# Waits of a few turns, shared products in a gradient, and the dealing out of expert units in a hand-scheduled two-layer network

## The chip, the cores and the metric

The kernel runs on one core of one Trainium2 chip. The metric is the device time of one execution in microseconds (us). The kernel before takes 3922.72 us, the median of three runs (3920.65 to 3936.18). All shares and durations below come from one further execution with the profiler, which took 3921.06 us.

## What is computed

Two residual layers over x of 16 sequences by 512 tokens by 128 features, in float32. Each layer normalises its input once and adds two branches to it:

```python
x = x + memory(xn) + block(xn)            # layer 0, xn = layernorm(x)
x = x + attention2(xn) + moe32(xn)        # layer 1
```

- `memory`: a neural memory. Keys k and values v come from the tokens. Over eight chunks of 64 tokens, one after the other, a two-layer network (w0, w1, and a norm weight ln) predicts v from k; its loss is differentiated by hand, the gradient is clipped to norm 1 over all parameters, and the parameters take a step with momentum. Then all tokens are read out through the final network.
- `block`: a convolution over three tokens, attention with 16 heads of 8 features (not causal), a layernorm, and eight dense experts of width 512, all applied to all tokens and weighted by a softmax gate.
- `attention2`: causal attention, a convolution over its output whose result is used as queries for a second causal attention with the same keys and values, and a projection.
- `moe32`: 32 experts of width 96, the best eight per token, with a capacity of 128 tokens per expert.

With the forward pass y = h w1ᵀ, r = 1/rms(y), ŷ = y r, pred = k + ŷ ln, and e = (pred - v) = ŷ ln + (k - v), the gradient of a chunk needs, per token (th is the token's step weight):

```
for y:   r * th * (e*ln - ŷ * mean(e*ln*ŷ))
for ln:  sum over tokens of th * e * ŷ
```

## The kernel before

The work of all sequences and both layers is cut into generators (`norm0`, `scan`, `front0`, `tops`, `back`, `post0`, `ffn`, `middle`, `front1`, `between`, `last`, `moe`). The class `Turns` runs them: in each **turn** every live generator goes on to its next `yield`, in the order of a priority number (`tops` is 0, `back` 1, the memory 3, the rest 4 to 6). Instructions are issued in that order, and TensorE (PE) keeps it; the other engines' orders are the scheduler's. The last argument of `idle(n)` is a number of turns, and a transfer or a chain on slow engines is covered by idling.

- `largest` (lines 371 to 420, in `tops`) computes the attention scores of a sequence and half of the heads once, only for the row maxima: per turn eight or fewer matmuls into one PSUM tile `s`, and VectorE (DVE) takes the maximum into `nm` (L396, or L387 with the causal mask). There is one such tile, so the next turn's matmuls (`s<-kx,qx`) wait for DVE. In the causal case the rows of keys are 512, 384, 256 and 128 wide; the two narrow ones put two or four heads into a turn and add the mask on the last 128 columns in two additions (L395) before the maximum. DVE instructions of later priority stand behind the maximum of their turn.
- The maxima go through DRAM (`top`) into extra rows of `qx`. `back` starts `lag` turns after `tops` has marked this, computes the scores anew with the maxima subtracted (`s<-qx,kx`), exponentiates on ScalarE (ACT), masks on GpSimd (POOL, L471) and sums against the values (`pc<-e,vp`).
- `ffn(b)` (line 511) runs the dense experts of sequence b as 64 **units**: `first` is a matmul `phe` with its relu, `second` four matmuls into `pye`. A credit of TURN minus the modelled load of the turn's other matmuls, at most 4000, buys units at 1000 each; with `pairs` only even numbers are taken, and none or four while the values of a turn are being summed. At the start it loads `ac`, `x1T` and expert 0's weights, and idles two turns.
- `fill` (line 195) puts a matmul without use into a turn whose PE load is light, if no unit was due in the last two turns.
- `scan` is the memory: `project(c)` makes keys and values of a chunk, `step(c)` a chunk's update. In it `gradient(q)` treats one half of the tokens (L860 to L898: L878 on POOL, L880 to L894 on DVE, L897 on ACT), the halves starting at turns 7 and 11 of the step. `norm_gradient` (L900) starts at turn 16 and makes the products for ln over all tokens on POOL (L904 to L910) in the buffer `gy`, which it shares with the loaded tokens `xc` of a chunk. `readout(b)` starts every six turns once the steps are done; `rq` goes through POOL (L1000, L1001) before PE transposes it, and its `yq` lies in the one buffer `hT1` until its sum is stored.
- Layer 1 starts when the scan is done; turns are counted from `t0`, 44 per sequence. `middle(b)` needs `ffn(b)` done, `front1(b)` loads `xT`, which `middle` has stored to DRAM just before, and idles two turns.
- All plain transfers are issued from SyncE's (SP's) queue, in order: one that waits holds up those behind it.

```python
credit[0] = min(credit[0] + TURN - load_ns[0], 4000)
n = int(max(credit[0] + 500, 0) // 1000)
if pools["pairs"]:
    n = n // 2 * 2 if "values" not in locks or n > 3 else 0
```

Of the kernel before, what the change touches and what calls it, by code (L numbers as in the profile page):

```python
# [17 lines left out]
P = 128  # L18
# [13 lines left out]
NTILE = N // P  # L32
BASE_LR = 0.01

TURN = 2750

ARRAY = 860
SCALE = 1.0 / float(np.sqrt(DH))
# [35 lines left out]
def bc(ap, axis, n):  # L74

    u = ap.unsqueeze(axis)
    shape = list(u.shape)
    shape[axis] = n
    return u.to_broadcast(shape)
# [3 lines left out]
def network(ctx: ExitStack, tc: tile.TileContext, a, out):  # L83
# [181 lines left out]
    def idle(n):  # L265
        for _ in range(n):
            yield
# [102 lines left out]
    def largest(slot, causal):  # L370


        q, k, at = slot
        yield from acquire("p1")
        nm = att.tile([P, TB, 2, NH], F32, tag="nm", bufs=2, name="nm")
        for i, n, per, t in widths(causal):
            qt = TB - 1 - i
            s = pools["ps"].tile([P, 2, 512], F32, tag="p1", bufs=pools["p1"], name="s1")
            sv = s[:, :, 0 : per * n].rearrange("p r (i n) -> p r i n", i=per)
            for u in range(per):  # L380
                for r in range(2):
                    rr = slice(64 * r, 64 * r + 64)
                    mm(sv[:, r, u, :], q[rr, t + u, qt * P : (qt + 1) * P], k[rr, t + u, :n])
            if causal and per == 1:

                for r in range(2):
                    newest[0] = nc.vector.tensor_tensor_reduce(  # L387
                        out=sv[:, r, 0, :], in0=sv[:, r, 0, :], in1=row["caus"][:, S - n :], scale=1.0, scalar=-BIG,
                        op0=ALU.add, op1=ALU.max, accum_out=nm[:, qt, r, t : t + 1],
                    )  # L390
            else:
                if causal:
                    for r in range(2):
                        dg = sv[:, r, :, n - P : n]
                        nc.vector.tensor_tensor(dg, dg, bc(row["caus"][:, S - P :], 1, per), ALU.add)  # L395
                newest[0] = nc.vector.tensor_reduce(nm[:, qt, :, t : t + per], sv, AX.X, ALU.max)  # L396
            yield
        locks.remove("p1")
        padded = maxima.pop(0)
        maxima.append(padded)  # L400
        mp = padded[:, 0 : TB * 16].rearrange("p (t r i x) -> p t r i x", t=TB, r=2, i=2)
        nc.vector.tensor_scalar(mp[:, :, :, 0, :].bitcast(FR), nm, -1.0, None, ALU.mult)
        nc.vector.scalar_tensor_tensor(
            mp[:, :, :, 1, :].bitcast(FR), nm, -1.0, mp[:, :, :, 0, :], ALU.mult, ALU.subtract
        )
        yield
        yield from room()

        tp = work("tpm")
        nc.tensor.transpose(tp[:, 0:P], padded, ident)  # L410
        m = att.tile([TB * 16, P], FR, tag="m", bufs=1, name="m")
        nc.scalar.copy(m, tp[0 : TB * 16, 0:P])
        nc.sync.dma_start(at, m.bitcast(F32))
        at = at.rearrange("(a r i t) s -> r i t a s", r=2, i=2, t=NH)
        for r in range(2):
            rows = q[64 * r + 32 : 64 * r + 34, :, :].bitcast(F32)
            nc.sync.dma_start(rows.rearrange("i t (a s) -> i t a s", s=P), at[r])
        yield
# [87 lines left out]
        mm(o[:, 0 : S - 1], w(2), src[:, 1:S], start=False)  # L506


    credit = [0.0]

    def ffn(b):

        yield from after(("x1", b))
        ac = ff.tile([P, TB, D], F32, tag="x1", bufs=1, name="ac")
        nc.sync.dma_start(flat(ac), x1d[0, b])
        x1T = ff.tile([P, S], F32, tag="x1T", bufs=1, name="x1T")
        nc.sync.dma_start(x1T, x1d[1, b])
        w1, w2 = {}, {}

        def fetch1(e):  # L520
            w1[e] = ff.tile([P, DFF], F32, tag="ew1", bufs=2, name="ew1")
            nc.sync.dma_start(w1[e], a["ew1"][:, e, :])

        def fetch2(e):
            w2[e] = ff.tile([P, 4, D], F32, tag="ew2", bufs=2, name="ew2")
            nc.sync.dma_start(w2[e], a["ew2"][:, e])

        fetch1(0)
        fetch2(0)
        yield from idle(2)  # L530
        pr = sm.tile([P, TB, EXP0], F32, tag="pr", bufs=2, name="pr")
        prT = ff.tile([EXP0, S], F32, tag="y", bufs=2, name="prT")

# [31 lines left out]
            nc.gpsimd.tensor_tensor(ac, ac, y, ALU.add)  # L565
            yield

        hs, pye = {}, [None]

        def first(i):  # L570
            e, f = divmod(i, 4)
            if e + 1 < EXP0 and f < 2:
                (fetch1, fetch2)[f](e + 1)
            ph = work("phe")
            mm(ph, w1[e][:, f * P : (f + 1) * P], x1T)
            hs[i] = ff.tile([P, S], F32, tag="hTe", bufs=3, name="hTe")
            nc.scalar.activation(hs[i], ph, AF.Relu, bias=col("fb", i))  # L577

        def second(i):
            e, f = divmod(i, 4)  # L580
# [12 lines left out]
                nc.gpsimd.tensor_tensor(ac, ac, y, ALU.add)  # L593
                drop()

        n = 4 * EXP0
        units = [(first, 0)]
        for i in range(1, n):
            units += [(first, i), (second, i - 1)]
# [2 lines left out]
        while at < len(units):  # L602

            at_ffn[0] = clock[0]
            credit[0] = min(credit[0] + TURN - load_ns[0], 4000)
            n = int(max(credit[0] + 500, 0) // 1000)
            if pools["pairs"]:
                n = n // 2 * 2 if "values" not in locks or n > 3 else 0
            for fn, u in units[at : at + n]:

                if held[0] >= pools["work"] - (fn is second and u % 4 == 0):
                    break
                fn(u)
                at += 1
                credit[0] -= 1000
            next(gating, None)
            yield
# [139 lines left out]
    def scan(s1):  # L757
# [47 lines left out]
        def step(c):  # L805
# [1 line left out]
            k, kv = ks.pop(c)  # L807

            eb = s1.tile([P, 2 * INTER + D], F32, tag="eb", name="eb")
            ln2 = sm.tile([P, D], F32, tag="ln2", bufs=2, name="ln2")  # L810

            def before():
                nc.gpsimd.tensor_tensor(ln2, ln, ln, ALU.mult)
                yield from idle(4)
                for s_, m_, lo, hi in ((surp, mem, 0, 2 * INTER), (sln, ln, 2 * INTER, 2 * INTER + D)):
                    nc.gpsimd.tensor_scalar(s_, s_, eta[:, c : c + 1], None, ALU.mult)
# [44 lines left out]
            def gradient(q):  # L861


                a4 = slice(4 * q, 4 * q + 4)
                yield from room()
                py = toks(work("py"))
# [8 lines left out]
                gt = s1.tile([P, 2, 4, D], F32, tag=f"hT{q}", name="gt")  # L875
                gq, tq = gt[:, 0], gt[:, 1]
                g[q] = gq
                nc.gpsimd.tensor_tensor(tq, kv[:, a4, :], bc(ln, 1, 4), ALU.mult)  # L878
                yield from idle(3)
                nc.vector.tensor_tensor(yq, yq, bc(ry[:, a4], 2, D), ALU.mult)  # L880
                nc.gpsimd.tensor_tensor(tr[:, a4], ry[:, a4], th[:, a4, c], ALU.mult)
                yield
                nc.vector.tensor_tensor(gq, yq, bc(ln2, 1, 4), ALU.mult)
                yield
                nc.vector.tensor_tensor(gq, gq, tq, ALU.add)
                yield
                nc.vector.tensor_tensor(tq, gq, yq, ALU.mult)
                yield
                nc.vector.tensor_reduce(m[:, a4], tq, AX.X, ALU.add)
                nc.vector.tensor_scalar(m[:, a4], m[:, a4], -1.0 / D, None, ALU.mult)  # L890
                yield
                nc.vector.tensor_tensor(tq, yq, bc(m[:, a4], 2, D), ALU.mult)
                yield
                nc.vector.tensor_tensor(gq, gq, tq, ALU.add)  # L894
                yield
                for t in range(4):
                    nc.scalar.mul(gq[:, t, :], gq[:, t, :], tr[:, 4 * q + t : 4 * q + t + 1])  # L897
                yield  # L898

            def norm_gradient():  # L900

                yield from after(("read", c + 1) if c + 1 < NC else ("read", c))
                gy = late["gy"] = s1.tile([P, NT, D], F32, tag="gy", name="gy")
                nc.gpsimd.tensor_tensor(gy, yh, bc(ln, 1, NT), ALU.mult)  # L904
                yield
                nc.gpsimd.tensor_tensor(gy, gy, kv, ALU.add)
                yield
                nc.gpsimd.tensor_tensor(gy, gy, yh, ALU.mult)
                yield
                nc.gpsimd.tensor_tensor(gy, gy, bc(th[:, :, c], 2, D), ALU.mult)  # L910
                yield

            def back(q):
# [11 lines left out]
                (0, before()), (0, turned(kT, lambda t: k[:, t, :], 0)), (1, turned(kT, lambda t: k[:, 4 + t, :], 1)),  # L925
                *[(1 + q, hidden(q)) for q in range(4)],
                *[(4 + 2 * q + i, hidden_turned(q, i)) for q in range(2) for i in range(2)],
                (7, gradient(0)), (11, gradient(1)), (16, norm_gradient()),
            )
            dyT = s1.tile([P, NT * P], F32, tag="kT", name="dyT")  # L930
            yield from timed(
# [58 lines left out]
        def readout(b):  # L990
# [8 lines left out]
            rms_rows(rq, q, TB, s1)  # L999
            nc.gpsimd.tensor_tensor(q, q, bc(row["qn"], 1, TB), ALU.mult)  # L1000
            nc.gpsimd.tensor_tensor(q, q, bc(rq, 2, D), ALU.mult)  # L1001
            yield from idle(3)
            yield from room()
            qT = s1.tile([P, S], F32, tag="sg", bufs=2, name="qT")
            transpose_tokens(qT, q)
# [18 lines left out]
                for i in range(2):  # L1024
                    mm(py[:, t, :], hT[:, i, t * P : (t + 1) * P], w1T[:, i, :], start=(i == 0), stop=(i == 1))
            ry = sm.tile([P, TB], F32, tag="r_yq", name="r_yq")
            y = s1.tile([P, TB, D], F32, tag="hT1", name="yq")
            nc.scalar.copy(y, py)
            rms_rows(ry, y, TB, s1)
            yield from idle(3)  # L1030
# [55 lines left out]
        mark("tops", layer, b, i, c)  # L1086

    def back(layer, b, i, c):
        yield from after(("tops", layer, b, i, c), lag=4)
        yield from after(("vals", layer, b))  # L1090
        z = live[layer, b]
        if c == 0:
            z["cn"] = (l1 if layer else fa).tile([P, TB, D], F32, tag="cn", bufs=2, name="cn")
        yield from weighted(z[i, c], z["vp"], c, layer == 1, z["cn"], ("back", layer, b, i, c))
# [129 lines left out]
    def front1(b):  # L1224
# [3 lines left out]
        z = live[1, b] = {"vp": got[0]}  # L1228
        xT = l1.tile([P, S], F32, tag="st", bufs=2, name="xT")
        nc.sync.dma_start(xT, xt[1, b])  # L1230
        yield from idle(2)
        for n, order in (("q", (0, 0, 1, 1)), ("k", (0, 1, 0, 1))):
            yield from room()
            pj = hold("pj" + n)
# [219 lines left out]
        nc.sync.dma_start(out_b[b], x1)  # L1454
        yield

    TBB, t0 = 44, max(turns.turn, 480)

    def begun(b, i, c):

# [132 lines left out]
```

## Time and profile before

| | |
|---|---|
| median of three runs | 3922.72 us |
| profiled execution | 3921.06 us |
| its span, first to last instruction | 3919.1 us |
| mean granted PE clock | 0.960 |
| fills: matmuls and their time | 238 matmul records, 122.5 us |
| transfers of SP's queue | 359.73 MB, 32.1% of 16 DMA engines |

The page gives each engine's busy time and its share of the span, and the span in 40 slices with a digit for the busy tenths. A float32 matmul leaves two records, so counts of PE are about twice those of the code. A group row reads: line, engine, operation, result <- operands, shapes, count, then busy time, mean ns of one, and the idle time of the engine just before, with what ended it. A row of waits reads: engine and what waited <- what ended the wait: total us, times, longest. A row of windows gives start and end, length, busy time and count of PE, of its weight loads (PEld), of DVE, ACT and POOL, then the granted clock of PE, the share of the DMA engines and GB/s.

Placed over the trace by the order of PE's instructions, the start takes until 110 us, the memory's eight steps until about 1288 us (turn 400), the readout until 1585 us (turn 482), layer 1 with the last dense experts until 3480 us (turn 1127), and the sparse experts with the last attention the rest. There are 1276 turns.

### The profile page before, as it was taken

What the parts mean: (1) busy time and instruction counts of PE and PEld (TensorE: products, weight loads), DVE (VectorE), ACT (ScalarE), POOL (GpSimd) and SP (SyncE); (2) the same over time, 40 slices, a digit from 0 to 9 for tenths busy, and PEclk for the clock granted to TensorE, in tenths of its full rate; (3) what the DMA queues carried; (4) which work ended last, traced back from release to release, by engine and by line L of the source; (5) the groups of instructions that cost most, each with busy time, mean ns of one, the idle gap of its engine ahead of it and who ended that gap; (6) DMA issues with size and microseconds to landing.
All of it is one profiled execution on the core that took longest, in us unless ns stands there. A gap on an engine that the chain in (4) does not pass through costs nothing. (4 is left out here: it accounts for less than half of the span.)

```text
span 3919.1 us, 62028 instructions
## 1 busy us (share of the span) xinstructions
PE 3463.3 (88%) x22267; PEld 1898.2 (48%) x22267; DVE 2389.2 (61%) x5187; ACT 2152.6 (55%) x3687; POOL 1658.1 (42%) x2562
## 2 busy tenths in 40 slices
PE   5889888889899888999999999999999999987877
PEld 2445444445444444445555555555555555543343
DVE  5666646665665545546466666666666666667762
ACT  1555655665566666555555555555555555543443
POOL 5433542453342544323344344424443344333674
PEclk7999999999999999999999999999999999998998
DMA  5222212221322332433434433443334333433343
GB/s 159 64 64 70 67 51 80 64 67 39 106 69 87 95 86 77 128 87 104 123 94 117 113 112 102 110 122 111 104 107 121 107 113 101 120 97 84 83 91 86
DMA packets 289938, 370.50 MB, mean 95 GB/s; under 512 B 46008, under 2 KB 141408, under 8 KB 289248
## 3 DMA queue, kind: packets, MB, share of 16 engines
q1 hardware_dynamic: 282464, 359.73, 32.1%
q0 software_dynamic: 7168, 6.82, 1.1%
q8 instruction: 176, 2.88, 0.3%
q14 instruction: 130, 1.06, 0.1%
HBM read 236.59 MB, written 133.25 MB: 94 GB/s over the span
## 5 line engine op out<-in xcount | busy, mean ns | idle before, releaser
L467 ACT ACTIVATE e<-s 128x1024 f32<-128x1024 f32 (+1 forms) x1216 | 1190.7, 979 | 702.7 <-PE s L192 637.0
L396 DVE TENSOR_REDUCE nm<-s 128x2 f32<-128x1024 f32 (+1 forms) x704 | 861.2, 1223 | 683.9 <-PE s L192 676.3
L387 DVE CUSTOM_DVE_ANT_0 s<-s,sb_const 128x512 f32<-128x512 f32 (+1 forms) x1024 | 647.6, 632 | 543.1 <-PE s L192 524.3
L471 POOL TENSOR_SCALAR_AFFINE_SELECT e<-e 128x128 f32<-128x128 f32 (+2 forms) x1408 | 467.8, 369 | 1003.2 <-ACT e L467 1000.9
L192 PE MATMUL s<-kx,qx 64*128 64x512 f32 (+3 forms) x3072 | 622.0, 432 | 236.8 <-DVE nm L396 132.1
L192 PEld LDWEIGHTS s<-kx,qx 64*128 64x128 f32 x3072 | 275.2, 188 | 895.6 <-issue 275.3
L192 PE MATMUL pc<-e,vp 128*32 128x512 f32 (+3 forms) x6144 | 642.3, 506 | 26.9 <-POOL e L471 26.5
L585 PEld LDWEIGHTS pye<-ew,hTe 128*128 128x128 f32 x4096 | 514.7, 195 | 141.4 <-issue 126.0
L585 PE MATMUL pye<-ew,hTe 128*128 128x128 f32 x4096 | 581.7, 286 | 0.8 <-DMA ew<-in_ew 0.8
L577 ACT ACTIVATE hTe<-phe,sb_cols 128x512 f32<-128x512 f32 x512 | 353.7, 691 | 404.7 <-PE phe L192 402.8
L192 PE MATMUL phe<-x1T,ew 128*128 128x512 f32 x1024 | 538.4, 610 | 14.1 <-DMA x1T<-x1d 6.7
L192 PE MATMUL s<-qx,kx 64*128 64x512 f32 (+3 forms) x3072 | 511.3, 359 | 34.3 <-ACT e L467 25.7
L593 POOL TENSOR_TENSOR ac<-ac,y 128x512 f32<-128x512 f32 x128 | 164.8, 1288 | 399.7 <-ACT y L592 397.4
L192 PEld LDWEIGHTS s<-qx,kx 64*128 64x128 f32 x3072 | 290.3, 190 | 77.1 <-ACT e L467 54.6
L395 DVE TENSOR_TENSOR s<-s,sb_const 128x256 f32<-128x256 f32 (+1 forms) x384 | 199.9, 521 | 150.8 <-PE s L192 138.4
L192 PEld LDWEIGHTS pc<-e,vp 128*32 128x32 f32 x6144 | 151.9, 110 | 255.8 <-issue 172.9
L192 PEld LDWEIGHTS phe<-x1T,ew 128*128 128x128 f32 x1024 | 160.2, 196 | 32.4 <-issue 8.2
L592 ACT ACTIVATE y<-pye,pr 128x128 f32<-128x128 f32 x512 | 146.6, 369 | 42.7 <-PE pye L585 37.9
L387 DVE DVE_READ_ACCUMULATOR2_ANT nm<- 128x1 f32 x1024 | 144.7, 141 | 0.0
L199 PE MATMUL fill<-sb_pb,sb_const 128*128 128x512 f32 (+2 forms) x238 | 122.5, 603 | 10.8 <-DMA sb_pb<-in_pb 10.4
L205 POOL TENSOR_SCALAR rs_t<-ss 128x4 f32<-128x4 f32 (+1 forms) x56 | 12.0, 215 | 197.4 <-ACT sq L258 195.8
L967 POOL TENSOR_TENSOR cl<-cl,phalf 128x1 f32<-128x1 f32 x8 | 4.5, 568 | 190.1 <-ACT cl L966 190.1
(294 smaller groups left out, 3991.8 us busy)
## 6 DMA issues: line engine op xcount, KB each, us to landing
ew<-in_ew SPq DMA_DIRECT2D x256, 256.0 KB
kx<-rk SPq DMA_DIRECT2D x192, 256.0 KB
qx<-rq SPq DMA_DIRECT2D x128, 256.0 KB
rq<-hi SPq DMA_DIRECT2D x64, 256.0 KB
rq<-lo SPq DMA_DIRECT2D x64, 256.0 KB
rk<-hi SPq DMA_DIRECT2D x64, 256.0 KB
rk<-lo SPq DMA_DIRECT2D x64, 256.0 KB
qx<-r SPq DMA_DIRECT2D x64, 256.0 KB
```

The costliest lines, as they stand in the source:

```text
L192: nc.tensor.matmul(o, lhsT=lhsT, rhs=rhs, start=start, stop=stop)
L199: nc.tensor.matmul(o[:, 0:n], lhsT=ident, rhs=cell[0][:, 0:n], start=True, stop=True)
L205: nc.gpsimd.tensor_scalar(t, src, scale, eps, ALU.mult, ALU.add)
L387: newest[0] = nc.vector.tensor_tensor_reduce(out=sv[:, r, 0, :], in0=sv[:, r, 0, :], in1=row["caus"][:, S - n :], scale=1.0, scalar=-BIG, ...
L395: nc.vector.tensor_tensor(dg, dg, bc(row["caus"][:, S - P :], 1, per), ALU.add)
L396: newest[0] = nc.vector.tensor_reduce(nm[:, qt, :, t : t + per], sv, AX.X, ALU.max)
L467: nc.scalar.activation(e[:, :, 0 : per * n], s[:, :, 0 : per * n], AF.Exp, scale=SCALE)
L471: cleared[0] = nc.gpsimd.affine_select(out=ev[:, r, :, 0:P], in_=ev[:, r, :, 0:P], pattern=[[0, per], [1, P]], compare_op=ALU.is_ge, fill= ...
L577: nc.scalar.activation(hs[i], ph, AF.Relu, bias=col("fb", i))
L585: nc.tensor.matmul(pye[0][:, t, :], lhsT=h[:, t * P : (t + 1) * P], rhs=w2[e][:, f, :], start=(f == 0 and t == 0), stop=(f == 3), skip_gro ...
L592: nc.scalar.mul(y[:, t, :], pye[0][:, t, :], pr[:, t, e : e + 1])
L593: nc.gpsimd.tensor_tensor(ac, ac, y, ALU.add)
```

## The change

- TURN falls from 2750 to 2700.
- The two mask additions of a turn become one of twice the size.
- `fetch0(b)` loads `x1T` and expert 0's weights. It is called when the last `first` of the sequence before has been issued, if the input of the next is ready; only the first sequence fetches for itself, and idles three turns.
- The gradient forms e = ŷ ln + (k - v) once per half, and both results use it: e·ŷ is written into `gy` (for ln, then scaled by th on POOL) and times ln into the mean; e·ln takes the rest. The products of `norm_gradient`, of `ln2` and of (k - v)·ln go; the second half starts at turn 9 instead of 11, and the scaling on ACT one turn later.
- `readout` idles five turns for `rq` instead of three, and its `yq` lies in the buffer of its own hidden values (`h` or `ds`).
- `back` waits five turns behind `tops` instead of four, `front1` three for `xT` instead of two, and `t0` is 480 instead of the turn in which the scan ended, if that is later.

```diff
-TURN = 2750
+TURN = 2700
...
-                    for r in range(2):
-                        dg = sv[:, r, :, n - P : n]
-                        nc.vector.tensor_tensor(dg, dg, bc(row["caus"][:, S - P :], 1, per), ALU.add)
+                    dg = sv[:, :, :, n - P : n]
+                    nc.vector.tensor_tensor(dg, dg, bc(bc(row["caus"][:, S - P :], 1, per), 1, 2), ALU.add)
...
+    def fetch0(b):
+
+        x1T = ff.tile([P, S], F32, tag="x1T", bufs=1, name="x1T")
+        nc.sync.dma_start(x1T, x1d[1, b])
+        fetched[b] = x1T, {}, {}
+        fetch1(*fetched[b][1:], 0)
+        fetch2(*fetched[b][1:], 0)
...
-        fetch1(0)
-        fetch2(0)
-        yield from idle(2)
+        if b not in fetched:
+            fetch0(b)
+            yield from idle(3)
+        x1T, w1, w2 = fetched.pop(b)
...
+            if i == n - 1 and ("x1", b + 1) in done:
+                fetch0(b + 1)
...
-                nc.gpsimd.tensor_tensor(ln2, ln, ln, ALU.mult)
...
-                nc.gpsimd.tensor_tensor(tq, kv[:, a4, :], bc(ln, 1, 4), ALU.mult)
...
-                nc.vector.tensor_tensor(gq, yq, bc(ln2, 1, 4), ALU.mult)
-                yield
-                nc.vector.tensor_tensor(gq, gq, tq, ALU.add)
-                yield
-                nc.vector.tensor_tensor(tq, gq, yq, ALU.mult)
-                yield
+                nc.vector.tensor_tensor(gq, yq, bc(ln, 1, 4), ALU.mult)
+                yield
+                nc.vector.tensor_tensor(gq, gq, kv[:, a4, :], ALU.add)
+                yield from after(("read", c + 1) if c + 1 < NC else ("read", c))
+                if q == 0:
+                    late["gy"] = s1.tile([P, NT, D], F32, tag="gy", name="gy")
+                gy = late["gy"][:, a4, :]
+                yield
+                nc.vector.tensor_tensor(gy, gq, yq, ALU.mult)
+                yield
+                nc.vector.tensor_tensor(tq, gy, bc(ln, 1, 4), ALU.mult)
+                yield
+                nc.gpsimd.tensor_tensor(gy, gy, bc(th[:, a4, c], 2, D), ALU.mult)
                 nc.vector.tensor_reduce(m[:, a4], tq, AX.X, ALU.add)
                 nc.vector.tensor_scalar(m[:, a4], m[:, a4], -1.0 / D, None, ALU.mult)
                 yield
+                nc.vector.tensor_tensor(gq, gq, bc(ln, 1, 4), ALU.mult)
+                yield
                 nc.vector.tensor_tensor(tq, yq, bc(m[:, a4], 2, D), ALU.mult)
-                yield
                 nc.vector.tensor_tensor(gq, gq, tq, ALU.add)
+                yield
                 yield
...
-            def norm_gradient():
-
-                yield from after(("read", c + 1) if c + 1 < NC else ("read", c))
-                gy = late["gy"] = s1.tile([P, NT, D], F32, tag="gy", name="gy")
-                nc.gpsimd.tensor_tensor(gy, yh, bc(ln, 1, NT), ALU.mult)
-                yield
-                nc.gpsimd.tensor_tensor(gy, gy, kv, ALU.add)
-                yield
-                nc.gpsimd.tensor_tensor(gy, gy, yh, ALU.mult)
-                yield
-                nc.gpsimd.tensor_tensor(gy, gy, bc(th[:, :, c], 2, D), ALU.mult)
...
-                (7, gradient(0)), (11, gradient(1)), (16, norm_gradient()),
+                (7, gradient(0)), (9, gradient(1)),
...
-            yield from idle(3)
+            yield from idle(5)
...
-            y = s1.tile([P, TB, D], F32, tag="hT1", name="yq")
+            y = s1.tile([P, TB, D], F32, tag=("h", "ds")[b % 2], name="yq")
...
-        yield from after(("tops", layer, b, i, c), lag=4)
+        yield from after(("tops", layer, b, i, c), lag=5)
...
-        yield from idle(2)
+        yield from idle(3)
...
-    TBB, t0 = 44, max(turns.turn, 480)
+    TBB, t0 = 44, 480
```

More of the change, by code (lines that the diff above doesn't have):

```diff
@@ L506, in conv, with fetch1, fetch2 @@
         mm(o[:, 0 : S - 1], w(2), src[:, 1:S], start=False)
-    credit = [0.0]
+    credit, fetched = [0.0], {}
+    def fetch1(w1, w2, e):
+        w1[e] = ff.tile([P, DFF], F32, tag="ew1", bufs=2, name="ew1")
+        nc.sync.dma_start(w1[e], a["ew1"][:, e, :])
+    def fetch2(w1, w2, e):
+        w2[e] = ff.tile([P, 4, D], F32, tag="ew2", bufs=2, name="ew2")
+        nc.sync.dma_start(w2[e], a["ew2"][:, e])
+    def fetch0(b):
[4 more added lines that the diff above has]
+        fetch2(*fetched[b][1:], 0)
     def ffn(b):
@@ L515, in ffn @@
         nc.sync.dma_start(flat(ac), x1d[0, b])
[L516 to L526, printed above, removed]
-        fetch1(0)
-        fetch2(0)
-        yield from idle(2)
+        if b not in fetched:
+            fetch0(b)
+            yield from idle(3)
+        x1T, w1, w2 = fetched.pop(b)
         pr = sm.tile([P, TB, EXP0], F32, tag="pr", bufs=2, name="pr")
@@ L566, in gate @@
             yield
-        hs, pye = {}, [None]
+        hs, pye, n = {}, [None], 4 * EXP0
         def first(i):
@@ L572, in first @@
             if e + 1 < EXP0 and f < 2:
-                (fetch1, fetch2)[f](e + 1)
+                (fetch1, fetch2)[f](w1, w2, e + 1)
             ph = work("phe")
@@ L594, in second @@
                 drop()
-        n = 4 * EXP0
         units = [(first, 0)]
@@ L605, in ffn @@
             credit[0] = min(credit[0] + TURN - load_ns[0], 4000)
-            n = int(max(credit[0] + 500, 0) // 1000)
+            more = int(max(credit[0] + 500, 0) // 1000)
             if pools["pairs"]:
-                n = n // 2 * 2 if "values" not in locks or n > 3 else 0
-            for fn, u in units[at : at + n]:
+                more = more // 2 * 2 if "values" not in locks or more > 3 else 0
+            for fn, u in units[at : at + more]:
                 if held[0] >= pools["work"] - (fn is second and u % 4 == 0):
@@ L809, in step @@
             eb = s1.tile([P, 2 * INTER + D], F32, tag="eb", name="eb")
-            ln2 = sm.tile([P, D], F32, tag="ln2", bufs=2, name="ln2")
             def before():
-                nc.gpsimd.tensor_tensor(ln2, ln, ln, ALU.mult)
                 yield from idle(4)
@@ L891, in gradient @@
                 yield
+                nc.vector.tensor_tensor(gq, gq, bc(ln, 1, 4), ALU.mult)
+                yield
                 nc.vector.tensor_tensor(tq, yq, bc(m[:, a4], 2, D), ALU.mult)
+                nc.vector.tensor_tensor(gq, gq, tq, ALU.add)
                 yield
-                nc.vector.tensor_tensor(gq, gq, tq, ALU.add)
                 yield
```

## The prediction

> **What bounds it now.** I read the page first, the busy line and the slices:
>
> ```profile
> PE 3463.3 (88%) x22267; PEld 1898.2 (48%) x22267; DVE 2389.2 (61%) x5187; ACT 2152.6 (55%) x3687; POOL 1658.1 (42%) x2562
> ...
> PE   5889888889899888999999999999999999987877
> ...
> PEclk7999999999999999999999999999999999998998
> ```
>
> TensorE (PE) is the bound throughout: 456 us of the span of 3919.1 are left idle, and no other engine passes 61%. The page's chain of work that ended last covers only the last 43 us (indirect scatters, final copies), so it can't price the middle. A gain has to come out of PE's idle time, its fill matmuls, or its clock. Second, PE's waits over the whole span ("waited for: total us, times, longest"):
>
> ```profile
> PE s L192 <- DVE nm L396: 132.1, 145, 5.9
> ...
> PE pjq L192 <- DMA xT<-xt: 11.5, 7, 5.0
> ...
> PE tp L244 <- POOL rq L1001: 9.8, 4, 4.7
> ...
> PE s L192 <- DMA qx<-top: 7.8, 5, 2.7
> PE phe L192 <- DMA x1T<-x1d: 6.7, 1, 6.7
> ...
> PE pgt L192 <- DMA x1T<-x1d: 4.3, 2, 3.5
> PE tp L244 <- ACT yq L1028: 4.3, 1, 4.3
> PE ppq L192 <- ACT yq L1028: 4.2, 1, 4.2
> ```
>
> Each of these rows stands in front of something that the diff edits. Third, the windows behind single waits; PEclk is the granted clock, next to last but two:
>
> ```profile
> 1646.00:1658.00 12.00, 6.17 (x12) 2.40 (x13) 4.23 (x16) 2.74 (x3) 0.00 (x0) 0.59 0.40 130
> 1676.00:1686.00 10.00, 3.45 (x6) 1.55 (x6) 0.85 (x1) 1.63 (x2) 0.00 (x0) 0.66 0.94 274
> ...
> 2560.00:2570.00 10.00, 7.96 (x54) 3.75 (x57) 6.39 (x28) 3.10 (x4) 2.08 (x6) 0.83 0.63 206
> ```
>
> Here PE waited 5.04 us (from 1645.9, xT), 6.74 us (from 1675.8, x1T) and 1.82 us (from 2560.4, xT). Afterwards part of the window runs at a lower clock: (1 - 0.59) x 12 = 4.9 us, 3.4 us and 1.7 us are lost on top. So a wait of about 2 us or more is paid nearly twice. The mean clock of 0.960 says that this loss is 157 us in all.
>
> **Transfers** (lag 4 to 5; xT three turns ahead instead of two; x1T and expert 0's weights fetched by the batch before). The rows: 11.5 + 6.7 + 4.3 + 7.8 = 30.3 us of idle; the clock loss behind the six longest, from windows like the above, 4.9 + 3.4 + 3.4 + 1.8 + 1.7 + 1.7 = 17; together 47. A turn of this stage lasts 2.92 us on average, more than every xT and top wait but the 5.04, of which about 2 us stay. x1T now starts when the last `phe` matmul of the batch is through, not behind SyncE's (SP's) wait for the accumulator's store. In the new order of SP's instructions it stands ahead of that store. I take 35 of 47. The added waits: `lag` delays the weighting of each pair of heads by one turn, which only keeps a score slot longer; the turns in which score rows are produced stay the same in the order of instructions, up to the last, and the end comes one turn later (1277 turns for 1276): +2.
>
> A rule speaks against counting the clock: the Trainium skill (TensorE: Matmul & The Clock Gate, HAM oscillation) says to avoid PE gaps above about 3.4 us, and the wait at 2560 of 1.82 us is followed by 0.83 all the same. By the rule only the waits of 5.04, 6.74 and 3.45 us would lose clock, 12 us in place of 17. The measurement decides; I keep 17.
>
> **Readout** (five idle turns instead of three; `y` in the tile of its own hidden values instead of the single hT1). Rows: 9.8 + 4.3 + 4.2 and smaller ones behind yq of 2.4, 20.7 us; clock loss in the five windows 1326:1340, 1399:1412, 1438:1452, 1488:1498, 1550:1566: 3.4 + 3.4 + 3.4 + 1.7 + 5.1 = 17. Of 38 I take 30. Two more turns give POOL some 7 us more; the wait for a tile whose store is pending goes, as its next user comes some nine turns later. What the turns cost: the scan ends at turn 486 instead of 482, which is hidden by the attention of layer 0, whose turns run on; layer 1's first rows are ready at turn 513 instead of 507 and are used from 544.
>
> **Gradient.** The longest waits for the maxima (nm) lie here. The timeline at 597 us, with start, duration, engine, line:
>
> ```profile
> 597.41 2.68 POOL L906 TENSOR_TENSOR gy<-gy,v 128x1024 f32<-128x1024 f32 x1
> ...
> 597.80 2.84 DVE L883 TENSOR_TENSOR gt<-yh,ln 128x512 f32<-128x512 f32 x1
> ...
> 600.57 1.21 DVE L396 TENSOR_REDUCE nm<-s 128x2 f32<-128x1024 f32 x1
> ...
> 601.83 0.50 PE L192 MATMUL s<-kx,qx 64*128 64x512 f32 x2 [2.32 <-DVE nm L396]
> ```
>
> and the groups of VectorE (DVE) in 110 to 1288 us (busy, mean ns, then idle before):
>
> ```profile
> L883 DVE TENSOR_TENSOR gt<-yh,ln 128x512 f32<-128x512 f32 x16 | 28.7, 1794 | 0.0
> ...
> L920 DVE TENSOR_TENSOR ds<-ds,pdh 128x512 f32<-128x512 f32 x32 | 21.5, 677 | 0.0
> ```
>
> A product of two SBUF tiles takes 0.68 us alone and up to 2.84 us beside a product on POOL; one with an operand in PSUM (L920) stays at 0.68. The maxima queue behind it, and PE behind them. The change removes POOL's L904 to L908 (19.9 + 21.5 + 21.5), L910 (17.3), L878 (21.3) and L813 (3.6): 105 us; it adds 16 scalings of 512 elements at 1.06 us (the row of L1001), 17. DVE's six products per quarter cost 115.4 us over 96 calls, 1.20 each; now there are eight, 128 calls at between 0.68 and 1.20: 87 to 154. I take 0.80, as projection's POOL products (L797 to L801) still collide. What this frees on PE: the eight longest stalls of the stage (185, 202, 332, 444, 600 to 607, 737, 1007, 1131) sum to 30 us, and 19 more of clock; a wait of 3.98 us at 872 behind the scaling on ScalarE (L897, which now gets one more turn) with 1.7 of clock; 55 in all. Against it: the second half starts at turn 9 instead of 11, so both chains stand in DVE's queue for some eight turns of a step. At 0.68 the new order puts at most 2.5 us between two maxima in a running step, which with 1.22 for the maximum exceeds a turn's 3.3. I take 25 of 55.
>
> **Mask.** Two additions become one. By the rows L395, two of 256 elements (0.43 each) become one of 512 (0.70), two of 512 one of 1024 (1.22, the reduce's row): 0.17 us off DVE's chain per turn, 192 turns. In 121 of them a PE gap ends with this chain, at most 20 us; I take 10.
>
> **Experts.** I cut both instruction orders into turns, counted the units and gave the counts the mean times of before. Turns 540 to 1120: 284 without a unit (2.53 us), 233 with two (2.93), 63 with four (4.67); after 279, 242, 59: 1695.4 against 1690.5, -5. The same for turns 110 to 540: -13. The last unit moves from turn 1125 to 1133: turns 1120 to 1145 get 12 more units, +4; -14 together. Twelve fills fewer (119 to 107; 122.5 us / 119 = 1.03 each) all lay in the empty turns between batches, which shrink from 5 to 8 to 3 to 6. Since some of those idle times are counted above, -13 for the whole. TURN's 2% alone moves little, because units go out in pairs.
>
> **New waits.** A shifted order draws its accidental waits anew. Those of before that the change doesn't aim at (4.59 us at 286, 2.23 us at 554, each with 3.4 of clock) make 13.6; I add 13.
>
> **Sum**: -35 + 2 - 30 - 25 - 10 - 13 + 13 = -98. Against the profiled execution (3921.06 us, 2 more than its span) 3823; the median shown lies 1.7 higher: **3825 us**.
>
> **Rivals.** *The waits return elsewhere*: half of each term survives, since DVE's queue or the next transfer is only a little less late: about 3870. For it: PE's waits for nm L396 number 145, most of them short and untouched. *More comes true*: 47 + 38 + 55 + 20 + 14 + 12 (fills) with nothing new, less 2, make 184: 3739; no row speaks for a schedule without new waits, but 3780 is half-way. *It does not do what it says*: pairs make TURN's change void and the batches' ends are all that move: that loses only the 13, 3838. *Slower, SP's queue*: the prefetch puts a wait for the last `phe` and for weights into SP's in-order queue, ahead of score rows. SP already waits 297.5 us in 55 times for PE phe before L522, 5.4 each. If each of 15 boundaries then delayed rows by 5.4 us plus 3.4 of clock, 132 us would come against the 98: 3957. It decides as soon as the rows' slack of three turns (9 us) is used up; against it, waits of scores for rows in the body are only 7.8 us though such fetches stand there now.
>
> **Numbers.** Forecast (3780 to 3850) 0.55, waits return (3850 to 3903) 0.25, more comes true (below 3780) 0.10, SP's queue 0.10, half of it within 0.5% where it takes only the gains. A difference under 0.5%, about 20 us, can't be told from none. Range 3765 to 3900. Faster 0.90, same 0.05, slower 0.05.
>
> **What would show it.** Right: the rows pjq <- xT, phe and pgt <- x1T, tp <- rq and yq nearly gone; L904 to L908 gone and the gradient's products near 0.7 to 0.8 us; nm L396's total below 110; clock above 0.965; no fills between turns 486 and 1120. Wrong: qx <- top or kx <- rk rows growing (SP), or DVE's products still above 1.1 us with longer nm waits in 110 to 1288.

## The result and the profile after

The changed kernel takes 3925.77 us (median of 12 runs, 3913.82 to 3939.58), the kernel before 3924.97 us on the same chip (12 runs, 3920.51 to 3936.45). The ratio is 1.0002 with a 95% interval of 0.9987 to 1.0017: no change, where 3825 us was forecast. Below, a ratio is always to the kernel before on the same chip, and a difference of two ratios is turned into time with 3925 us; by the intervals given, such a difference is uncertain by about 11 us.

The page of the changed kernel: busy line, PE's slices, granted clock.

```profile
span 3922.9 us, 61837 instructions
...
PE 3459.9 (88%) x22243; PEld 1893.7 (48%) x22243; DVE 2319.1 (59%) x5027; ACT 2156.4 (55%) x3687; POOL 1576.6 (40%) x2522
...
PE   5999789889899898999999999889998989888877
...
PEclk7999899999999999999999999999999999997999
```

DVE lost 70 us of work and POOL 81, as the change meant, and nothing came of it: PE is idle for 463 us, as before (456), and the mean granted clock is 0.957 where a rise above 0.965 was expected. PE's waits over the whole span say where it went:

```profile
PE s L192 <- DVE nm L395: 135.7, 134, 6.3
PE s L192 <- DVE nm L387: 36.6, 52, 1.5
PE s L192 <- issue: 35.8, 22, 2.4
...
PE s L192 <- DMA kx<-rk: 27.8, 5, 15.8
...
PE phe L192 <- DVE lo L326: 15.9, 10, 4.9
...
PE pjq L192 <- DMA xT<-xt: 1.6, 2, 1.2
...
PE s L192 <- DMA qx<-top: 1.4, 2, 1.0
...
PE tp L244 <- ACT yq L1027: 0.8, 1, 0.8
```

The rows that the change aimed at did go: xT from 11.5 to 1.6 us, top from 7.8 to 1.4, yq from two rows of 4.3 and 4.2 to one of 0.8; x1T and rq through POOL have no row left. But the waits for the maxima (nm) hardly fell (the reduce's row is 135.7 us for 132.1 before, that of L387 36.6 for 57.5), "issue" in front of `s` grew from 5.2 to 35.8, and `kx<-rk` from 10.1 to 27.8. Cut by turns, the loss has a place: turns 640 to 1120, where layer 1 runs evenly, took 1399 us before and take 1443 after (PE idle 100 and 137), while turns 400 to 540 gained 43 us.

### The profile page after: what moved, and what is told of

It is laid out like the page before. It is cut to its first block, busy times and chain, and to the rows that moved or that the text cites. A ratio compares the mean times of both kernels' runs of the same rounds, so it can differ in the third digit from the quotient of the medians.

```text
span 3922.9 us, 61837 instructions
## 1 busy us (share of the span) xinstructions
PE 3459.9 (88%) x22243; PEld 1893.7 (48%) x22243; DVE 2319.1 (59%) x5027; ACT 2156.4 (55%) x3687; POOL 1576.6 (40%) x2522
## 5 line engine op out<-in xcount | busy, mean ns | idle before, releaser
L395 DVE TENSOR_REDUCE nm<-s 128x2 f32<-128x1024 f32 (+1 forms) x704 | 861.5, 1224 | 641.3 <-PE s L192 634.0
L387 DVE CUSTOM_DVE_ANT_0 s<-s,sb_const 128x512 f32<-128x512 f32 (+1 forms) x1024 | 647.0, 632 | 520.5 <-PE s L192 503.3
L192 PE MATMUL s<-kx,qx 64*128 64x512 f32 (+3 forms) x3072 | 625.5, 433 | 258.3 <-DVE nm L395 135.7
L192 PE MATMUL pc<-e,vp 128*32 128x512 f32 (+3 forms) x6144 | 666.2, 522 | 31.0 <-POOL e L470 30.7
L394 DVE TENSOR_TENSOR s<-s,sb_const 128x512 f32<-128x512 f32 (+1 forms) x192 | 168.4, 877 | 258.1 <-PE s L192 257.5
L387 DVE DVE_READ_ACCUMULATOR2_ANT nm<- 128x1 f32 x1024 | 144.7, 141 | 0.0
L199 PE MATMUL fill<-sb_pb,sb_const 128*128 128x512 f32 (+2 forms) x214 | 107.2, 590 | 10.0 <-DMA sb_pb<-in_pb 9.9
L205 POOL TENSOR_SCALAR rs_t<-ss 128x4 f32<-128x4 f32 (+1 forms) x56 | 11.5, 205 | 237.1 <-ACT sq L258 235.9
L205 POOL TENSOR_SCALAR rs_t<-ln_mv 128x4 f32<-128x4 f32 x64 | 13.2, 206 | 168.4 <-DVE ln_mv L215 165.9
```

What stands on the lines that cost most here:

```text
L192: nc.tensor.matmul(o, lhsT=lhsT, rhs=rhs, start=start, stop=stop)
L199: nc.tensor.matmul(o[:, 0:n], lhsT=ident, rhs=cell[0][:, 0:n], start=True, stop=True)
L205: nc.gpsimd.tensor_scalar(t, src, scale, eps, ALU.mult, ALU.add)
L387: newest[0] = nc.vector.tensor_tensor_reduce(out=sv[:, r, 0, :], in0=sv[:, r, 0, :], in1=row["caus"][:, S - n :], scale=1.0, scalar=-BIG, ...
L394: nc.vector.tensor_tensor(dg, dg, bc(bc(row["caus"][:, S - P :], 1, per), 1, 2), ALU.add)
```

## The experiments

Three theories were held against each other. **Theory 1**: `lag` 5 lays the turns that sum values, which get no expert units, onto the wrong places of layer 1's cycle. **Theory 2**: the one large mask addition makes the chain in front of the maxima worse. **Theory 3**: TURN 2700 hands out too few units.

Layer 1's scores for the maxima come in a cycle of 11 turns: places 0 to 3 are 512 keys wide, 4 to 7 are 384, 8 and 9 are 256 with two heads, 10 is 128 with four. Four of the 11 turns also sum values. This is the changed kernel's timeline at places 8, 9 and 10 (start, duration, engine, line, instruction, and in brackets the idle time before it):

```profile
2602.40 0.50 PE L192 MATMUL s<-kx,qx 64*128 64x256 f32 x4
...
2602.95 0.70 DVE L394 TENSOR_TENSOR s<-s,sb_const 128x512 f32<-128x512 f32 x1 [1.40 <-PE s L192]
2603.07 0.65 PE L192 MATMUL pc<-e,vp 128*32 128x128 f32 x16
2603.68 1.22 DVE L395 TENSOR_REDUCE nm<-s 128x4 f32<-128x1024 f32 x1
2605.05 0.50 PE L192 MATMUL s<-kx,qx 64*128 64x256 f32 x4 [1.34 <-DVE nm L395]
...
2610.02 0.66 PE L192 MATMUL s<-kx,qx 64*128 64x128 f32 x8
...
2610.72 1.23 DVE L394 TENSOR_TENSOR s<-s,sb_const 128x1024 f32<-128x1024 f32 x1 [3.17 <-PE s L192]
2611.99 1.23 DVE L395 TENSOR_REDUCE nm<-s 128x8 f32<-128x1024 f32 x1
...
2613.32 0.50 PE L192 MATMUL s<-kx,qx 64*128 64x512 f32 x2 [2.35 <-issue]
```

At 2602.40 a turn with two heads begins: addition and maximum keep DVE until 2604.90. Beside it PE has the narrowest sum (128 columns, 0.65 us) and, since values are summed, no unit: it stands for 1.34 us. At 2610.02 the turn with four heads has neither sum nor units beside it (27 of the 44 turns at this place do get units): 2.35 us, called "issue", though the maximum ended only 0.1 us before the next `s`. Over the 43 cycles of this stage place 8 lasts 2.67 us with 1.58 of PE work; before it lasted 3.40 with 2.99.

**Undoing the lag alone.**

```diff
-        yield from after(("tops", layer, b, i, c), lag=5)
+        yield from after(("tops", layer, b, i, c), lag=4)
```

> The changed kernel with the lag of back at 4 turns again. Theory 1 (alignment): the lag of 5 put the unit-free turns that sum the values on the turn whose scores are 256 wide, where DVE's chain is longest; with 4 they are back on the last 384-wide turn. Layer 1's body, turns 640 to 1120, falls from 1143 us to about 1100 (before: 1099), the cycle of 11 turns from 33.3 to about 32 us; the whole is about 3875 (some 45 less than the changed kernel, 5 given back because the last units end at turn 1140 and there are 1281 turns for 1277). Theory 2 (one wide mask addition lengthens DVE's chain) and theory 3 (TURN and the prefetch deal the units out worse): the body stays at 1135 to 1150, the whole within 10 us of 3926.

Where this text and the next say 1143, 1100 and 1099 us for turns 640 to 1120, read 1443, 1400 and 1399, as above. Measured: 0.9766 (0.9747 to 0.9784), 3842.04 us. One number in one line is worth 93 us, twice what was expected: the rest of the change gains 92 us, and the lag gives all of it back. The timeline with lag 4, same places:

```profile
2605.14 0.40 PE L192 MATMUL s<-qx,kx 64*128 64x512 f32 x2
2605.47 0.64 PE L192 MATMUL pc<-e,vp 128*32 128x128 f32 x16
2606.68 0.50 PE L192 MATMUL s<-kx,qx 64*128 64x256 f32 x4 [0.57 <-DVE nm L387]
...
2612.35 0.66 PE L192 MATMUL s<-kx,qx 64*128 64x128 f32 x8
2612.82 0.42 PE L192 MATMUL s<-qx,kx 64*128 64x384 f32 x2
2613.16 1.92 PE L192 MATMUL pc<-e,vp 128*32 128x512 f32 x16
```

Now the narrowest sum stands beside a maximum of 384 keys and costs 0.57 us, and the widest (1.92 us) covers the chain of the four heads. By place, over all cycles of turns 640 to 1120: the columns of the sum in the turn, and PE's mean idle time between the turn's work and the next turn's, in us.

| Place | keys, heads | lag 4: sum, idle | lag 5: sum, idle |
|---|---|---|---|
| 0 | 512, one | none, 0.03 | 512, 0.00 |
| 1 | 512, one | none, 0.01 | none, 0.10 |
| 2 | 512, one | none, 0.24 | none, 0.09 |
| 3 | 512, one | 384, 0.00 | none, 0.22 |
| 4 | 384, one | none, 0.03 | 384, 0.01 |
| 5 | 384, one | 256, 0.00 | none, 0.00 |
| 6 | 384, one | none, 0.04 | 256, 0.00 |
| 7 | 384, one | 128, 0.40 | none, 0.02 |
| 8 | 256, two | none, 0.32 | 128, 1.09 |
| 9 | 256, two | none, 0.09 | none, 0.12 |
| 10 | 128, four | 512, 0.28 | none, 0.85 |

Places 8 and 10 hold what is new: 1.94 us a cycle for 0.60.

**The lag alone, in the kernel before**: the same line the other way, 4 to 5, nothing else.

> The kernel before with the lag of back at 5 turns and nothing else. Theory 1: the body of layer 1 grows by 35 to 50 us, the whole to 3965 to 3985 (with 5 to 10 us for 1283 turns instead of 1276). Theories 2 and 3: the body stays within 10 us of before's 1099, the whole at 3920 to 3935, and the waits of scores for top (7.8 us) go.

Measured: 1.0269 (1.0248 to 1.0291). The lag's cost doesn't need the rest of the change; it was larger than expected (turns 640 to 1120 take 1493 us instead of 1399).

**Lag 6** in the changed kernel.

> The changed kernel with a lag of 6. In its order the unit-free summing turns stand at places 1, 5, 7 and 9 of the cycle of 11, place 9 being the second 256-wide turn. Theory 1 (what counts is which turns are empty): a cycle of 32.5 to 33.5 us and a whole of 0.995 to 1.01 of before, no worse than the lag of 5 by more than its longer end (1288 turns, some 10 us). Rival (a longer lag is bad in itself, each turn of it costs the 80 us that 4 to 5 did): 1.02 or above.

Measured: 0.9941 (0.9922 to 0.9961): better than 5, worse than 4. A longer lag isn't worse by its length; where the sums fall decides more. With 6 the narrowest sum lies on place 9, still a turn with two heads (2.65 us with 1.38 of PE work), so theory 1 explains why it stays behind 4; that it beats 5 fits its units on place 8 (3.62 us with 3.45), but wasn't tested further.

**The lag in one layer only.** In the first run layer 0 has 5 and layer 1 has 4, in the second the reverse.

```diff
-        yield from after(("tops", layer, b, i, c), lag=5)
+        yield from after(("tops", layer, b, i, c), lag=(5, 4)[layer])
```

> The changed kernel with lag 5 in layer 0 and lag 4 in layer 1. Theory 1 (the places in layer 1's cycle of eleven turns): nearly all of the gain of lag 4 is back, a ratio of 0.977 to 0.982. Rival (a longer lag costs in both layers alike, by slots kept longer): about half, 0.988. If the memory's steps, 21 us longer with lag 5 in the profile, are lag's own doing, 0.982.

> The changed kernel with lag 4 in layer 0 and lag 5 in layer 1. Theory 1: nearly all of the loss stays, a ratio of 0.995 to 1.000, and the idle turn of 2.7 us with 1.5 us of PE's work stands at the first place of two heads of 256 in the cycle. Rival (lag costs in both layers alike): about 0.988.

Measured: 0.9910 (0.9889 to 0.9931) with 5 in layer 0, and 1.0016 (0.9999 to 1.0032) with 5 in layer 1. PE's waits in turns 640 to 1120, first with 5 in layer 0 only:

```profile
PE phe L192 <- DVE lo L326: 26.4, 9, 3.9
PE s L192 <- DVE nm L395: 9.7, 9, 1.9
PE pjq L192 <- DMA xT<-xt: 8.9, 4, 3.0
```

then with 5 in layer 1 only:

```profile
PE s L192 <- DVE nm L395: 57.5, 52, 1.3
...
PE s L192 <- issue: 19.2, 9, 2.4
```

The waits for the narrow maxima follow layer 1's lag (54.3 us in the changed kernel, 17.5 with lag 4 throughout, where the row "issue" is 1.1 us in all), and lag 5 in layer 1 alone brings the whole loss back. So theory 1 holds for layer 1. It isn't all, and its forecast for layer 0 (0.977 to 0.982) missed: layer 0's lag alone costs 57 us (0.9910 against 0.9766) by another way. Between the two profiled executions, 43 us apart, it costs 21 us in turns 110 to 400 and 40 us in turns 640 to 1120, and the other turns give back some 17. In turns 640 to 1120 a wait of `phe` for the low part `lo` of a projection recurs, 7 times of about 3.5 us and at most once per sequence, which has no row with lag 4, and the waits for `xT` are back. Why layer 0's lag moves these is open. The two lags don't add up: 57 and 98 singly, 93 together.

**Units in summing turns too**, with lag 5 and, as the control, with lag 4.

```diff
-                more = more // 2 * 2 if "values" not in locks or more > 3 else 0
+                more = more // 2 * 2
```

> The changed kernel, lag still 5, but units may go out two at a time in the turns that sum the values as well. The first 256-wide turn of the cycle then gets 1.41 units on average instead of none. Theory 1: its time rises by less than its PE work (it had 1.15 us of idle PE), the turns that lose units get shorter, the body falls from 1443 to about 1410 or less and the whole to 0.985 to 0.992 of before. Rival (the lag hurts in another way, by buffers or the queue of transfers): 0.998 or above.

> The changed kernel with lag 4 and with units also in turns that sum values (pairs, no minimum of four). Theory 1 (with lag 5 summing turns without units fall on the turns whose maxima take DVE longest): at lag 4 they do not, so units there have nothing to repair: within 0.5% of lag 4 alone, a ratio of 0.972 to 0.982, or worse. Rival (units in summing turns pay wherever these turns lie, so that the run with lag 5 showed nothing of the places): again some 1.4% better, 0.963.

Measured: 0.9864 (0.9842 to 0.9887) with lag 5, 54 us better than without; 0.9804 (0.9784 to 0.9825) with lag 4, 15 us worse than without. So units in these turns help only where the turns lie badly, which speaks for the places. The repair is partial: place 8 now lasts 3.09 us with 2.76 of PE work, but the units miss at place 9 (2.89 with 2.10), and in turns 640 to 1120 the row for nm L395 is 48.7 us against 54.3.

**Two mask additions again**, in the changed kernel and with lag 4.

```diff
-                    dg = sv[:, :, :, n - P : n]
-                    nc.vector.tensor_tensor(dg, dg, bc(bc(row["caus"][:, S - P :], 1, per), 1, 2), ALU.add)
+                    for r in range(2):
+                        dg = sv[:, r, :, n - P : n]
+                        nc.vector.tensor_tensor(dg, dg, bc(row["caus"][:, S - P :], 1, per), ALU.add)
```

> The changed kernel with the mask added in two additions again; nothing else, and the same order of PE. Theory 2 (the one addition cannot start until both halves' matmuls are through, the first of two can): 30 to 45 us faster than the changed kernel, about 3885, most of it in the body of layer 1. Theory 1: within 12 us of 3926, since the sum of both chains is nearly the same. Theory 3: the same as theory 1.

> The changed kernel with the lag at 4 and two mask additions. At a lag of 5 the one addition was worth 35 us in the body. Theory 1: the chain matters less where units cover the 256-wide turns, so two additions cost 5 to 15 us, 0.979 to 0.981 of before. Rival (a fixed gain per masked turn, whatever stands there): 30 us or more, 0.985.

Measured: 1.0065 (1.0048 to 1.0082) and 0.9841 (0.9820 to 0.9863). Theory 2 falls: the merged addition is worth 25 us with lag 5 and 29 with lag 4. Theory 1's forecasts (within 12 us, then 5 to 15) missed as well; the rival of the second run came nearest.

**TURN 2750**, in the changed kernel and with lag 4.

> The changed kernel with TURN at 2750. Theory 3 (the lower credit deals the units out worse): 30 to 45 us faster than the changed kernel. Theory 1: the alignment is unchanged, so the body's cycle stays at 33 us or above; the units end at turn 1103 instead of 1133, so that the last 30 turns are filled with useless matmuls and the whole is 5 to 15 us slower than 3926.

> The changed kernel with the lag at 4 and TURN at 2750. The lag alone gave 0.977 of the time before. If TURN's 2700 costs something of its own (it cost some 25 us at a lag of 5), this is at 0.970 or below. If it only hurt because of the crowded turns at a lag of 5, the whole is within 0.3% of 0.977, with the last unit at turn 1103 instead of 1140 and 11 fills more.

Measured: 0.9933 (0.9916 to 0.9950) and 0.9714 (0.9693 to 0.9735). TURN 2700 costs 27 and 20 us of its own, so theory 3 holds beside theory 1, not in place of it. In the profiled executions with lag 4, 2750 saves 13 us in turns 640 to 1120 and 23 after them, where the last unit lies in turn 1103 instead of 1140, and loses 16 in turns 110 to 400. The second is the fastest version found: 3820.27 us, ahead of both kernels.

**Lag 4 and one more part undone**: `gradient` and `norm_gradient` as before; `readout` with three idle turns and `yq` in hT1; no `fetch0` for the next sequence, two idle turns.

```diff
-            if i == n - 1 and ("x1", b + 1) in done:
-                fetch0(b + 1)
...
-            yield from idle(3)
+            yield from idle(2)
```

> The changed kernel with the lag at 4 and the gradient as it was before. If the new gradient earned what the prediction gave it (25 us, by shorter products on DVE): 0.983 of before, all of it in turns 110 to 400, with DVE's products at 1.2 us on average again. Rival: the gain is eaten by stalls that the new order of POOL and SP brings (scores waiting 13 to 16 us for rows): 0.975 to 0.979.

> The changed kernel with the lag at 4 and the readout as before (three idle turns, one buffer hT1). Prediction: its waits and the clock behind them were worth 30 us, so 0.984 of before, with the loss in turns 400 to 486 and the rows tp <- POOL rq and yq back. Rival: the shift of turns by the shorter scan (477 instead of 483) gives most of it back: 0.979 or below.

> The changed kernel with the lag at 4, where each sequence's experts fetch for themselves and idle two turns, as before. Predicted worth of the prefetch: some 15 us of waits and clock at x1T. With TURN at 2700 the last unit now ends at turn 1159 instead of 1140, so that layer 1's last sequence is late and there are 1302 turns for 1281: another 20 to 30 us, as the turns of the end last up to 3 us but some are nearly empty. In all 0.985 to 0.990 of before. Rival (SP's queue is held up by the prefetch, which costs as much as it gives): 0.978 to 0.982.

Measured, against 0.9766 with all three: the old gradient 0.9834 (0.9811 to 0.9856), so the new one is worth 27 us (the two profiled executions are only 7 us apart, so in which turns isn't shown); the old readout 0.9784 (0.9760 to 0.9808), 7 us, not to be told from nothing; no prefetch 0.9923 (0.9903 to 0.9944), 62 us. With the old readout the waits do return (8.9 us for rq through POOL, 7.7 in three rows for yq), but the row for nm L395 is 94.0 us instead of 107.4 and the program has 1274 turns instead of 1281. Without the prefetch it has 1302, the last unit lies in turn 1159 instead of 1140, and what follows turn 1200 takes 272 us instead of 222; its waits for x1T are only 0.8 us.

**A new stall.** All versions with the new gradient and lag 4 or 5 have one stall of 12.8 to 15.8 us near 440 us. The changed kernel, SP's wait and PE's next instruction:

```profile
SPq L1116 <- POOL x L237: 16.5, 1, 16.5
```

```profile
453.87 0.76 PE L192 MATMUL s<-kx,qx 64*128 64x512 f32 x1 [15.76 <-DMA kx<-rk]
```

SP stands 16.5 us at a store of x1, which waits for a layernorm on POOL, and the rows of keys are queued behind it. The store was put four turns later, with lag 4 and TURN 2750.

```diff
-        nc.sync.dma_start(x1d[0, b], flat(x1))
         yield from idle(4)
+        nc.sync.dma_start(x1d[0, b], flat(x1))
```

> The changed kernel with the lag at 4, TURN at 2750, and the store of x1 in post0 issued four turns later, behind its idle turns. In the changed kernel scores once waited 15.8 us for key rows (13 to 14 us with the lag at 4), because SP sat 16.5 us on this store, whose data POOL had not finished. Theory: that stall and its clock loss go, 15 to 25 us, 0.965 to 0.968 of before. Rival: the queue then sits on the next thing POOL owes; 0.971 as without it.

Measured: 0.9729 (0.9706 to 0.9752), the same as without (0.9714). It decides nothing: in SP's queue the store still stands between the same two loads, with a wait of 16.8 us, and PE's stall is 13.9 us (14.1 without). What its removal would give stays open. With the old gradient (lag 4), and in the kernel before, there is no such stall, so the 27 us of the new gradient are net of it.

## Why the prediction was wrong

The step that failed is the **lag**, priced at +2 us: "only keeps a score slot longer; the turns in which score rows are produced stay the same". Both halves are true and beside the point. The lag also decides in which turn the values are summed, these are the turns without units, and beside its scores the sum is nearly all that PE has there to cover DVE's chain. The table of the cycle, 11 places with their widths, sums and units, could have been drawn from the trace of before: the widest sum stood on the place of four heads, the narrowest on one of 384 keys, and one turn's shift moves both. It measured +93 us. The two profiled executions with lag 4 and 5 are 72 us apart, 66 of them in turns 640 to 1120, where PE is idle for 137 us instead of 88. In layer 1 the way is shown; how layer 0's lag costs, 57 us when it stands alone, stays open.

Without it the sum was nearly right, -100 forecast and -92 measured, but by luck, as a balance of terms that were off:

| Term | forecast, us | measured, us | by |
|---|---|---|---|
| lag | +2 | +93 | changed kernel against lag 4 |
| gradient | -25 | -27 | gradient undone, lag 4 |
| mask | -10, at most -20 | -29 (-25) | two additions with lag 4 (5) |
| readout | -30 | -7, uncertain | readout undone, lag 4 |
| TURN 2700 | about 0, in -13 | +20 (+27) | TURN 2750 with lag 4 (5) |
| prefetch | in -35 and -13 | -62 | prefetch left out, lag 4 |

The five lower rows add up to -105, not -92, so they aren't independent; the third idle turn for `xT` and `t0` were not run alone.

- *Transfers.* The waits went as said (30.3 us of rows are 3.0), but the prefetch's worth isn't its waits: without it the units end 19 turns later and the program has 21 turns more. The 17 us of clock were also too many, by some 3 us at the two longest waits: part of the lower clock lay inside them and cost nothing (1648.2 to 1650.95 us, granted clock 0.51, and 1679.0 to 1682.5 us, 0.50, with PE standing), so "paid nearly twice" was too strong.
- *Readout.* The rows went as said too; what they gave came back as waits for maxima and as turns. A row of waits says nothing of what was late next, and 30 of 38 was taken without looking for it.
- *Gradient.* The size came out right, in part by luck: the 27 us are net of the new stall near 440 us (13.0 us with lag 4), which the term did not have. The products' mean was foreseen as 0.80 us and is 0.81 (103.3 us for 128). In the groups of DVE in 110 to 1283 us (busy, mean ns) some still stand out, as L888 does beside L905; those of L888 with a product on POOL beside them take 1.12 us on average, the others 0.68:

```profile
L888 DVE TENSOR_TENSOR gt<-gt,v 128x512 f32<-128x512 f32 x16 | 16.2, 1009 | 0.0
...
L905 DVE TENSOR_TENSOR gt<-gt 128x512 f32<-128x512 f32 x16 | 10.9, 680 | 0.1
```

- *Mask.* The addition got shorter by what was foreseen (0.699 us against 2 x 0.43; 1.23 against 2 x 0.70). The bound of 20 us (121 gaps by 0.17) was about right and the half of it that was taken too little: behind these 192 turns PE stands for 59.0 us with one addition and 79.4 with two at lag 4 (65 and 126 gaps), for 120.6 and 143.4 at lag 5. So the waits gave 20 and 23 us; the rest of the 29 and 25 is within the uncertainty.
- *Experts.* The count of fills was right (107, none in turns 486 to 1120), but "TURN's 2% alone moves little" was wrong by 20 to 27 us. With lag 4 the profiled executions put more of that behind turn 1120 than in turns 640 to 1120; that fewer units per turn leave more turns to DVE's chain fits the second part (idle PE 88 us, 79 with 2750), and wasn't shown turn by turn.
- *New waits.* 13 us were added; the stall near 440 us alone is more than that, 15.8 us before what the clock loses after it.
- *Rivals.* "Waits return elsewhere" came nearest, but only in name: its 3870 kept half of each term, and the mechanism here is one edit against the rest. The marker against SP's queue did sound (`kx<-rk` 27.8 us), yet by the new gradient, not by the prefetch: the stall is gone with the old gradient and there without the prefetch (12.8 us).

## What to carry to other kernels

In a schedule dealt out by turns, a parameter that delays one stream by a turn changes which works share a turn; before it is priced at a latency, write out the cycle with each engine's work per place, before and after the shift, and take the longer engine at every place. Test each constant of a many-part change alone: here one line cancelled the 92 us that the rest gained, and a second (TURN) had already cost 20 of what that could have been. A wait that is removed is worth its row only if the next one is known to be early.

## What the runs showed of the hardware

After a gap of 2.35 us the clock fell: the widest sum after it (from 2613.92, the same 16 matmuls) took 2.78 us at a granted clock of 0.67 in that window, against 1.92 us at 1.00 with lag 4, where no gap stood in the 5 us before it. So a cycle that leaves such gaps can pay again on the work behind them, though not behind each: over turns 640 to 1120 the granted clock is 0.97 with lag 5 and 0.99 with lag 4, some 44 and 19 us of lost clock. The Trainium skill (TensorE: Matmul & The Clock Gate, HAM oscillation) warns of gaps above about 3.4 us; here the measurement decides, and after a shorter one the clock fell as well.
